# A two-layer graph kernel: the second product by one level of Strassen's algorithm, bias addition on GpSimd, 16 row tiles, and an explicit order of all steps

## The chip, the core and the metric

The kernel runs on one core of one Trainium2 chip. The metric is the device time of one execution in microseconds, as the median of several runs. A core has five engines that run side by side, each with its own in-order queue of instructions: TensorE (matmuls, results in PSUM), VectorE, ScalarE, GpSimd, and SyncE, which here only issues DMA transfers. Engines wait for each other through semaphores. In the profile they are PE (its weight loads are PEld), DVE, ACT, POOL and SP.

## What is computed

The input x has 32 batches of 512 rows by 1024 columns; adj is a 512x512 matrix; all is float32.

```python
h = jnp.maximum(_layernorm(x, axis=-1), 0.0)
x = x + _L0_gnn_ref(h, L0_gnn_wq, L0_gnn_wk, adj, L0_gnn_bm)
h = jnp.maximum(_layernorm(x, axis=-1), 0.0)
x = x + _L1_gnn_ref(h, adj, adj, L1_gnn_bias)
```

The first layer is an attention over the 1024 columns: scores are q[m] + k[n] through a leaky ReLU, a softmax over n, and the weighted sum of the columns, multiplied by adj and passed through a bias and a ReLU. The second is one dense product per batch, out[m, f] = sum over n of adj[n, m]^2 h[n, f], plus a bias per column f. The change concerns the second.

## The kernel before, in words

**Tiles.** A batch's 512 rows are four row tiles of 128 partitions by 1024 columns. They live in one pool, xp, with 18 buffers (ROWS). A batch takes twelve of them in the course of its life: four loads of x (load, L578), which become the normalised h in place and feed the first product; four reloads of x as y (reload, L583), which gather the residual sums and are stored at the end (L888); and four tiles of the second layer's h (relu, L613). A new tile waits until the buffer it is given is free: its last reader is done, and if it was stored, its store has landed.

**First layer.** value (L724) multiplies h by the transposed adjacency. Since the scores are a sum, the softmax sums are prefix sums over sorted columns: rank (L667, L672, L676, VectorE) counts each column's place, scatter (L736, L737, GpSimd) writes the columns in sorted order into a table in DRAM, fetch (L753) reads it back, stationary (L796, GpSimd), scan (L812) and sums (L821 to L828) make the prefix sums and write them back, and gather (L833, GpSimd) fetches for each column the three rows it needs. weigh (L858, ScalarE) and combine (L862, VectorE: sixteen 128x512 instructions per batch) put them together, and turn (L869, L871) transposes the result on TensorE and adds it to y on VectorE.

**Second layer.** stats (L591), norm and slopes make the layer norm of y, relu (L613) writes h. lift (L619, VectorE, four instructions) then adds the column bias to y. propagate (L876) makes eight results of 128x512 per batch (four row tiles c, two halves i of the columns), each a sum of four matmuls with the squared adjacency wsq (made once in square, L537). finish (L884, VectorE) adds each result and a per-row constant bm (which undoes the -bm that turn took as its lower limit) to y; after the second half of a row tile its store is issued on SyncE (L888).

**What sets the order.** Every function above is a step. A table (PLAN, with corrections for the first and last batches in FIRST and LAST) gives every step of every batch a time; the steps of all batches are sorted by it, and each engine's instructions stand in its queue in that order. Five or so batches are under way at once: one batch's propagate stands between another's scans and a third's values. PSUM has eight banks, one per result.

```python
for n, t in enumerate(times):
    t = s.b * T + t + shift + stretch * (t - mean)
    steps.append((t, len(steps), f, (s, *lead, *(args[n] if args else (n,)))))
...
steps.sort(key=lambda e: e[:2])
with tc.manual_schedule():
    for _, _, f, args in steps:
        f(*args)
```

Of the kernel before, what the change touches and what calls it, by code (L numbers as in the profile page):

```python
# [9 lines left out]
F32 = mybir.dt.float32  # L10
# [6 lines left out]
P = 128  # L17
# [8 lines left out]
ROWS = 18  # L26
QROWS = 4
PLAN = {
    "adjacency": (-988.26,),
    "biases": (-98.417,),  # L30
    "columns": (-36.55,),
    "combine": (
        258.562, 258.888, 261.232, 259.873, 259.273, 258.008, 255.401, 254.706, 263.584, 262.603,
        263.336, 256.739, 262.598, 262.619, 257.172, 258.38,
    ),
    "compare_mask": (-790.92,),
    "divide": (245.486,),
    "excess": (235.359,),
    "factors": (7.808,),
    "fetch": (33.445,),  # L40
    "finish": (320.504, 328.605, 338.372, 339.335, 347.583, 375.553, 352.541, 377.322),
    "from_rows": (59.35,),
    "gather": (219.377, 220.155, 219.449, 220.224, 220.347, 220.229, 219.664, 221.598),
    "later": (44.625,),
    "lift": (323.119, 320.65, 321.319, 325.518),
    "load0": (-153.915,),
    "load1": (-113.779,),
    "load2": (-165.384,),
    "load3": (-89.604,),
    "lower": (-8.757, 10.345, -12.887, -23.448, -21.118, -20.974, -1.148, 2.379),  # L50
    "masks": (-130.916,),
    "norm0": (-78.759,),
    "norm1": (284.555,),
    "pads": (-161.502, -74.73, -204.361, 23.867, -54.392),
    "propagate": (312.313, 317.412, 326.151, 316.354, 335.303, 344.312, 335.972, 347.511),
    "rank": (-14.187, -14.293, -17.198, -17.342, -15.511, -15.036, -11.325, -13.895),
    "reload0": (192.65,),
    "reload1": (238.382,),
    "reload2": (232.99,),
    "reload3": (257.454,),  # L60
    "relu0": (-61.287, -58.703, -61.202, -57.828),
    "relu1": (301.878, 303.027, 301.741, 302.05),
    "row": (-36.021,),
    "scan": (51.176, 57.633, 64.219, 81.673, 97.074, 108.292, 133.694, 146.062, 161.601),
    "scatter": (20.023, 15.884, 17.044, 17.539, 21.356, 19.535, 20.598, 20.763),
    "scores": (-41.613,),
    "slopes0": (-64.705,),
    "slopes1": (285.486,),
    "spread": (-28.707, -25.435, -27.151, -16.385, -9.829, -20.617, -16.323, -10.067),
    "square": (-559.865,),  # L70
    "stationary": (45.131, 68.681, 108.55),
    "stats0": (-97.083, -80.936, -91.631, -79.428),
    "stats1": (279.045, 280.054, 279.907, 280.042),
    "sums": (51.891, 59.593, 72.069, 86.019, 99.75, 116.792, 139.403, 150.307, 173.296),
    "to_rows": (-11.86, -7.955),
    "totals": (50.392,),
    "turn0": (264.575, 264.492, 264.401, 264.843),
    "turn1": (269.122, 269.027, 269.324, 268.845),
    "turn_adjacency": (-328.788,),
    "value": (-34.236, -39.683, -34.816, -23.667, -14.904, -27.47, -22.782, -17.741),  # L80
    "weigh": (250.503, 251.121, 249.656, 248.481, 251.121, 249.301, 250.914, 250.078),
    "weights": (41.352,),
}
FIRST = {
    "columns": (
        (-34.664, 0.5139), (-50.924, 3.8424), (-25.352, -0.3814), (5.756, -0.7592),
        (-3.834, -3.5685), (-13.836, 0.3613),
    ),
    "combine": (
        (-10.962, -0.1119), (-1.308, -0.1439), (3.109, -1.7623), (9.89, 2.7475), (4.44, -0.7933),  # L90
        (2.961, -1.451),
    ),
    "divide": (
        (-6.347, -0.8568), (2.891, -3.3805), (-4.843, -2.2912), (-14.719, 0.1095), (0.139, -0.7459),
        (-4.639, -1.4913),
    ),
    "excess": (
        (3.406, 3.0798), (0.53, -2.1584), (-5.407, -3.6123), (-5.253, 0.2855), (1.538, 1.0506),
        (-3.02, -0.7059),
    ),  # L100
    "factors": (
        (-39.948, -1.434), (8.997, -3.1502), (-4.905, 1.5535), (21.711, -1.2202), (-25.661, 2.8879),
        (13.506, 1.2709),
    ),
    "fetch": (
        (-7.266, -0.8474), (-8.348, -0.3577), (-7.803, -0.4204), (-12.929, 0.9352),
        (-3.76, -1.7209), (-5.744, 2.9838),
    ),
    "finish": (
        (-8.493, -0.4813), (6.16, 0.0186), (3.358, -0.186), (-1.573, -0.1421), (1.288, 0.2274),  # L110
        (-7.871, -0.1255),
    ),
    "from_rows": (
        (-0.341, 2.1537), (116.48, -0.09), (-35.198, 1.4406), (-25.171, -1.3726), (0.332, 0.6924),
        (-16.655, 0.2663),
    ),
    "gather": (
        (-5.507, 0.5725), (-4.646, -0.3848), (-17.558, -0.6343), (-8.351, -0.483), (5.293, 1.8179),
        (-2.911, -0.6571),
    ),  # L120
    "later": (
        (-10.16, 1.3573), (-2.311, -1.2079), (-2.744, 1.4084), (-11.928, 2.0169), (-8.624, -2.2893),
        (0.485, -2.4426),
    ),
    "lift": (
        (-13.784, -1.0616), (3.658, -0.7922), (-29.558, 1.5668), (-5.824, -1.5872), (1.316, 0.2108),
        (-13.838, -1.4015),
    ),
    "load0": (
        (-175.071, -1.0804), (-56.257, 0.2897), (-197.902, -2.8166), (2.16, -0.6659),  # L130
        (-45.079, 1.0239), (23.433, -0.0172),
    ),
    "load1": (
        (-99.914, 2.1645), (-71.298, -3.9416), (-78.407, 2.8558), (-85.073, 0.4063),
        (-18.406, -0.1573), (-28.218, 0.3374),
    ),
    "load2": (
        (-70.747, -1.2538), (-111.83, -0.5989), (-26.701, -0.4923), (-111.109, -0.0099),
        (-20.511, 0.9791), (15.469, 0.2457),
    ),  # L140
    "load3": (
        (-206.722, 1.2803), (-128.427, -0.9745), (-37.172, 1.9538), (-74.142, 0.1775),
        (-13.958, 1.1538), (-37.508, 0.7277),
    ),
    "lower": (
        (-27.213, -0.696), (-36.917, 0.5414), (-27.222, -0.2022), (-13.712, -0.526),
        (-10.212, -0.0938), (46.957, -1.0187),
    ),
    "norm0": (
        (-82.445, 1.5089), (-65.85, -1.4094), (-21.204, -0.8537), (-14.029, -0.5842), (1.32, 1.776),  # L150
        (1.134, -0.2082),
    ),
    "norm1": (
        (-3.753, -0.8553), (7.036, 1.1487), (-3.41, 0.1137), (10.96, 0.1134), (5.687, 1.1579),
        (-1.719, -1.6549),
    ),
    "propagate": (
        (-0.512, -0.1834), (1.688, 0.0269), (-2.93, -0.0228), (-0.493, -0.1178), (0.476, -0.1272),
        (0.797, -0.0815),
    ),  # L160
    "rank": (
        (-18.998, 0.7993), (-32.202, -0.2074), (-19.965, 1.145), (-3.668, -1.203),
        (-5.408, -1.0875), (2.158, -0.1924),
    ),
    "reload0": (
        (-78.853, -1.3542), (-2.901, -0.2085), (48.545, 0.1436), (11.898, 1.3227),
        (28.811, -1.2219), (-1.29, -0.8095),
    ),
    "reload1": (
        (-41.749, 0.1112), (-10.749, -0.6043), (11.812, -1.0105), (7.019, -0.2259),  # L170
        (-60.814, -0.4054), (-89.384, 1.1482),
    ),
    "reload2": (
        (5.935, 0.7012), (9.237, 1.9026), (-112.445, -1.6665), (29.821, 0.2364), (-22.535, -0.3722),
        (10.909, 1.7943),
    ),
    "reload3": (
        (-10.61, -1.1804), (-7.721, -1.5967), (-28.859, -3.3307), (-19.113, 0.0501),
        (-9.413, 0.4983), (-16.835, 0.7363),
    ),  # L180
    "relu0": (
        (-60.02, 1.4731), (-66.989, -0.4028), (-18.196, 0.1369), (-19.764, 0.0603), (3.168, 0.0151),
        (-1.522, 0.1367),
    ),
    "relu1": (
        (-11.851, 2.5102), (-0.995, 1.8084), (-17.155, -2.1914), (1.666, 2.1743), (4.982, -0.4455),
        (3.476, 0.1775),
    ),
    "row": (
        (-58.902, 0.8165), (-32.755, -3.2129), (-16.685, -0.2803), (-0.884, 2.3638),  # L190
        (-10.929, 0.751), (-15.002, 1.1386),
    ),
    "scan": (
        (-5.392, -0.0092), (-4.281, 0.0691), (-9.753, -0.1007), (-4.67, 0.0238), (-1.515, -0.0228),
        (-2.326, 0.0007),
    ),
    "scatter": (
        (-9.248, -0.2038), (-2.595, 1.766), (5.273, -0.6066), (-14.049, -0.0507), (0.917, 1.0603),
        (-5.17, -0.1987),
    ),  # L200
    "scores": (
        (-62.678, -1.1751), (-58.023, -2.2273), (-24.037, 0.8897), (-9.373, 1.8513),
        (-9.692, 0.3259), (-10.3, 1.643),
    ),
    "slopes0": (
# [765 lines left out]
```

## Time and profile before

| | |
|---|---|
| median of three runs | 2348.87 us (2348.57 to 2350.3) |
| the profiled execution | 2340.51 us, its span 2338.8 us |
| granted clock of TensorE | 0.994 on average |
| instructions | 27844 |
| DMA | 655.92 MB, mean 280 GB/s |
| HBM | 438.05 MB read, 215.99 MB written |

The profile is one execution. A row of the groups names the line, the engine, the operation and the tiles (out<-in) with their shapes and the number of instructions; then the busy time in us and the mean of one instruction in ns; then the engine's idle time just before these instructions, and who ended it. Instructions of one engine overlap a little at their ends, so the busy time of a group divided by its count is the pitch, somewhat below the mean. A row of the waits reads: who waited, for whom, us in total, times, the longest. In a timeline a row gives the start, the length in us, the engine and the instruction; equal ones that follow each other are one row with their count.

### The profile page before, as it was taken

How to read it: one execution, taken by the hardware profiler on the slowest of the kernel's cores; microseconds unless marked ns; L12 is line 12 of the kernel's file. 1: busy time of each engine (PE TensorE's matmuls, PEld its weight loads, DVE VectorE, ACT ScalarE, POOL GpSimd, SP SyncE). 2: the span in 40 equal slices, each digit the busy share in tenths (PEclk: the TensorE clock that was granted, in tenths of full speed). 3: DMA queues.
4: the chain of work that ended last, by engine and by line, in shares of the span. 5: the costliest groups of instructions: out<-in, count | busy, mean ns of one | idle time of the engine just before them, and what ended most of it. 6: DMA issues, size and time to landing. Idle time of an engine off the chain costs nothing.

```text
span 2338.8 us, 27844 instructions
## 1 busy us (share of the span) xinstructions
PE 2277.8 (97%) x7568; PEld 1001.3 (43%) x7568; DVE 1953.9 (84%) x4981; ACT 1445.1 (62%) x2821; POOL 740.0 (32%) x971
## 2 busy tenths in 40 slices
PE   7899999999999999999999999999999999999997
PEld 3334443444444444444444444444444444444343
DVE  6668897888898888898888898888988896899875
ACT  4677666565566665576665676665576656676530
POOL 2233323322323322324322323322323333334310
PEclk9999999999999999999999999999999999999998
DMA  5679878888888888888888888888787887787971
GB/s 194 236 272 332 286 250 290 299 295 280 271 295 293 306 284 294 267 298 294 304 283 293 270 299 294 303 292 299 251 311 262 313 301 280 259 296 274 328 291 78
DMA packets 205356, 655.92 MB, mean 280 GB/s; under 512 B 27504, under 2 KB 27632, under 8 KB 205200
## 3 DMA queue, kind: packets, MB, share of 16 engines
q1 hardware_dynamic: 141408, 360.37, 46.4%
q0 software_dynamic: 57344, 276.86, 30.8%
q10 hardware_dynamic: 6448, 16.92, 2.3%
q8 instruction: 61, 1.00, 0.2%
q14 instruction: 95, 0.78, 0.1%
HBM read 438.05 MB, written 215.99 MB: 280 GB/s over the span
## 4 chain that ended last, share of the span: by engine, by line
PE 85%; DVE 6%; DMA 4%; ACT 2%; issue 1%; POOL 1%; ACTq 0%; SPq 0%; DVEq 0%; POOLq 0%
PE pv L724 35%; PE pg L876 33%; PE sc L812 9%; PE tr L869 5%; PE pq L625 2%; DMA g<-td,idg 2%; DVE g L862 2%; DVE st L591 1%; PE sc L809 1%; POOL g L833 1%; ACT h L613 1%; DVE y L871 1%; DMA qd<-qr 1%; DVE junk L672 0%; ACT junk L683 0%
## 5 line engine op out<-in xcount | busy, mean ns | idle before, releaser
L876 PE MATMUL pg<-h,wsq 128*128 128x512 f32 x2048 | 905.3, 595 | 12.8 <-ACT h L613 12.8
L724 PE MATMUL pv<-wmT,x 128*128 128x512 f32 x2048 | 916.2, 598 | 0.0
L876 PEld LDWEIGHTS pg<-h,wsq 128*128 128x128 f32 x2048 | 384.2, 190 | 505.9 <-issue 464.3
L724 PEld LDWEIGHTS pv<-wmT,x 128*128 128x128 f32 x2048 | 377.1, 190 | 504.4 <-issue 442.7
L796 POOL TENSOR_TENSOR sm<-mask_a,wc 128x192 f32<-128x192 f32 x96 | 54.9, 572 | 1129.3 <-DVE wc L773 784.7
L821 ACT COPY vs<-sc 1x512 f32<-1x512 f32 x256 | 145.4, 568 | 374.8 <-PE sc L812 301.7
L862 DVE SCALAR_TENSOR_TENSOR g<-g,cf 128x512 f32<-128x512 f32 x512 | 360.9, 760 | 13.4 <-ACT g L858 10.6
L737 POOL DMA_INDIRECT td<-v,idx x256 | 290.5, 1135 | 236.0 <-POOL v L736 45.6
L683 ACT ACTIVATE junk<-qrow,qk 128x1024 uint8<-128x1024 f32 x256 | 294.1, 1149 | 11.9 <-DMA qrow<-qd 8.9
L833 POOL DMA_INDIRECT g<-td,idg x256 | 244.0, 953 | 125.2 <-issue 69.7
L812 PE MATMUL sc<-vs,sm 128*64 128x512 f32 x1024 | 265.9, 613 | 10.8 <-ACT vs L821 6.1
L884 DVE SCALAR_TENSOR_TENSOR y<-pg,bm_sb,y 128x512 f32<-128x512 f32 x256 | 186.0, 740 | 41.6 <-PE pg L876 26.8
L871 DVE SCALAR_TENSOR_TENSOR y<-tr,nbm,y 128x512 f32<-128x512 f32 x256 | 174.1, 742 | 38.5 <-PE tr L869 34.5
L824 ACT COPY t<-sc 128x512 f32<-128x512 f32 x288 | 168.3, 585 | 30.8 <-DMA td<-t 25.3
L672 DVE TENSOR_SCALAR_CACHE_REDUCE junk<-qrow,qk,cnt 128x512 uint8<-128x512 f32 (+6 forms) x224 | 180.4, 805 | 8.2
L667 DVE TENSOR_SCALAR_CACHE_REDUCE junk<-qrow,qk 128x512 uint8<-128x512 f32 (+6 forms) x224 | 165.4, 738 | 18.4 <-DMA qrow<-qd 13.3
L591 DVE BATCH_NORM_STATS2 st<-x 128x6 f32<-128x512 f32 x256 | 163.0, 678 | 17.7 <-DMA x<-in_x_dram 17.6
L858 ACT ACTIVATE g<-g,cf 128x512 f32<-128x512 f32 x256 | 163.2, 711 | 2.4 <-DVE cf L852 2.2
L613 ACT ACTIVATE h<-y,nmr,rstd 128x1024 f32<-128x1024 f32 x128 | 151.7, 1234 | 17.3 <-DMA out_dram<-y 9.4
L619 DVE TENSOR_TENSOR y<-y,bias_sb 128x1024 f32<-128x1024 f32 x128 | 151.3, 1213 | 12.0 <-ACT h L613 11.8
L591 DVE BATCH_NORM_STATS2 st<-y 128x6 f32<-128x512 f32 x256 | 159.3, 664 | 0.0
L731 ACT COPY v<-pv 128x512 f32<-128x512 f32 x256 | 139.0, 585 | 23.9 <-PE pv L724 9.9
(102 smaller groups left out, 1776.6 us busy)
## 6 DMA issues: line engine op xcount, KB each, us to landing
vs<-td SPq DMA_DIRECT2D x96, 792.0 KB
td<-t SPq DMA_DIRECT2D x576, 132.0 KB
x<-in_x_dram SPq DMA_DIRECT2D x128, 512.0 KB
y<-in_x_dram SPq DMA_DIRECT2D x128, 512.0 KB
out_dram<-y SPq DMA_DIRECT2D x128, 512.0 KB
qrow<-qd ACTq DMA_DIRECT2D x32, 512.0 KB
td<-v,idx POOLq DMA_INDIRECT x256, 4.9
g<-td,idg POOLq DMA_INDIRECT x256, 12.6
```

The lines of the kernel that those rows point to most:

```text
L591: nc.vector.bn_stats(st[:, i, :], s.x[c][:, ts(i, HALF)])
L613: nc.scalar.activation(h, s.x[c], AF.Relu, bias=s.nmr[:, c : c + 1], scale=s.rstd[:, c : c + 1])
L672: nc.vector.tensor_scalar(junk[:, j * P :], s.qrow[:, j * P :], qc, first, ALU.is_lt, ALU.add, accum_out=s.cnt[:, 1, j : j + 1],)
L683: nc.scalar.activation(junk, s.qrow, AF.Sign, bias=s.qk[:, 1, j : j + 1], accum_out=s.sgn[:, j : j + 1])
L724: nc.tensor.matmul(pv, s.h[c][:, ts(j, P)], wmT[:, c, :], start=(c == 0), stop=(c == NC - 1))
L737: i = nc.gpsimd.indirect_dma_start(tds[s.b % TABLES][:, :], bass.IndirectOffsetOnAxis(ap=s.idx[j // 4][:, j % 4 : j % 4 + 1], axis=0), v[: ...
L812: nc.tensor.matmul(p[ts(k, HP), :], m[:, k, :], s.vs[h][:, 0:C], start=True, stop=True)
L833: nc.gpsimd.indirect_dma_start(s.g[:, j, :], None, tds[s.b % TABLES].rearrange("(s k) w -> s k w", k=3), bass.IndirectOffsetOnAxis(ap=s.id ...
L862: nc.vector.scalar_tensor_tensor(r, s.g[:, j, k * W : k * W + C], s.cf[:, k, j : j + 1], r, ALU.mult, ALU.add)
L871: nc.vector.scalar_tensor_tensor(xh, pt, nbm[:, o : o + 1], xh, ALU.max, ALU.add)
L876: nc.tensor.matmul(pg, wsq[:, r, ts(c, P)], s.h[r][:, ts(i, HALF)], start=(r == 0), stop=(r == NC - 1),)
L884: nc.vector.scalar_tensor_tensor(xh, s.pg.pop((c, i)), bm_sb[:, c : c + 1], xh, ALU.add, ALU.add)
```

## The change

propagate no longer makes each 128x512 result from four matmuls. The 512x512 matrix, the rows and the column halves are split in two each, and Strassen's scheme in its form with shared sums makes the product from seven block products instead of eight. Each block product m is two half products u of two matmuls. square makes the combinations of the squared adjacency once (wmix, three of them; two blocks of wsq are overwritten). mix makes the combinations of h for every batch, in eight 128x512 subtractions on GpSimd, partly in place and partly in one more row tile, mx. Products 1, 6, 7 and 4 accumulate in one PSUM bank per u, products 5 and 3 in another, and finish reads the bank between them: seven instructions per u, four of which add bm. The store is a step of its own. lift goes from VectorE to GpSimd. ROWS goes from 18 to 16. PLAN, FIRST and LAST go, and a text (ORDER) names every step of the program in its order, two characters for each.

```diff
-ROWS = 18
+ROWS = 16
...
     def square(s):
         nc.gpsimd.tensor_tensor(wsq, s.adj, s.adj, ALU.mult)
+        a11, a21 = wsq[:, 0:2, 0 : C // 2], wsq[:, 0:2, C // 2 :]
+        a12, a22 = wsq[:, 2:4, 0 : C // 2], wsq[:, 2:4, C // 2 :]
+        s1, s2, s4 = wmix[:, 0], wmix[:, 1], wmix[:, 2]
+        nc.gpsimd.tensor_tensor(s1, a21, a22, ALU.add)
+        nc.gpsimd.tensor_tensor(s2, s1, a11, ALU.subtract)
+        nc.gpsimd.tensor_tensor(s4, a12, s2, ALU.subtract)
+        nc.gpsimd.tensor_tensor(a21, a11, a21, ALU.subtract)
+        nc.gpsimd.tensor_scalar(a22, a22, -1.0, None, ALU.mult)
+        forms.update({1: a11, 2: a12, 3: s4, 4: a22, 5: s1, 6: s2, 7: a21})
...
     def lift(s, c):
-        nc.vector.tensor_tensor(s.x[c], s.x[c], bias_sb, ALU.add)
+        nc.gpsimd.tensor_tensor(s.x[c], s.x[c], bias_sb, ALU.add)
...
+    def mix(s, k):
+        t, r = divmod(k, 2)
+        if k == 0:
+            s.mx = xp.tile([P, N], F32, tag="x", name=f"mx_{s.b}")
+        lo, hi = slice(0, HALF), slice(HALF, N)
+        d, h0, h1 = s.mx[:, ts(r, HALF)], s.h[r], s.h[2 + r]
+        out, one, two = (
+            (d, h0[:, hi], h0[:, lo]),
+            (h0[:, hi], h1[:, hi], h0[:, hi]),
+            (d, h1[:, hi], d),
+            (h1[:, lo], d, h1[:, lo]),
+        )[t]
+        nc.gpsimd.tensor_tensor(out, one, two, ALU.subtract)
+
+    def propagate(s, m, u):
+        row, i = {1: (0, 0), 2: (2, 0), 3: (2, 1), 4: (2, 0), 5: None, 6: None, 7: (0, 1)}[m] or (0, 0)
+        key = {1: 1, 6: 1, 7: 1, 4: 1, 5: 5, 3: 5, 2: 2}[m], u
+        if m in (1, 2, 5):
+            s.pg[key] = bank(f"pg_{s.b}_{m}_{u}")
+        for r in range(2):
+            data = s.mx[:, ts(r, HALF)] if m in (5, 6) else s.h[row + r][:, ts(i, HALF)]
             nc.tensor.matmul(
-                pg, wsq[:, r, ts(c, P)], s.h[r][:, ts(i, HALF)],
-                start=(r == 0), stop=(r == NC - 1),
-            )
...
+                s.pg[key], forms[m][:, r, ts(u, P)], data,
+                start=(m in (1, 2, 5) and r == 0), stop=(r == 1),
+                skip_group_check=True,
+            )
+
+    def finish(s, k, u):
+        key, c, i, last = (
+            (1, 0, 0, False), (2, 0, 0, True), (1, 0, 1, False), (5, 2, 1, True),
+            (1, 2, 1, False), (5, 0, 1, True), (1, 2, 0, True),
+        )[k]
+        xh = s.x[c + u][:, ts(i, HALF)]
+        if last:
+            nc.vector.scalar_tensor_tensor(
+                xh, s.pg[key, u], bm_sb[:, c + u : c + u + 1], xh, ALU.add, ALU.add
+            )
+        else:
+            nc.vector.tensor_tensor(xh, s.pg[key, u], xh, ALU.add)
+
+    def store(s, c):
+        nc.sync.dma_start(out[s.b, ts(c, P), :], s.x[c])
...
-    steps.sort(key=lambda e: e[:2])
+    names = list(lanes)
+    for code in ORDER.split():
+        for k in range(0, len(code), 2):
+            name, n = names[int(code[k : k + 2], 36)]
+            f, args = lanes[name, n].pop(0)
+            s, t = args[0], len(steps)
+            steps.append((t, len(steps), f, args))
```

In the middle of the new order (batches 8 to 20) each batch repeats the one before. A stretch of it, a step per word, the number after the point being the batch:

```
to_rows1.18 sums2.17 divide0.15 scatter6.18 propagate1.14 weigh4.15 scatter4.18 weigh7.15 combine8.15 propagate3.14 weigh6.15 load2.20 combine14.15 reload0.15 weigh5.15 scatter5.18 finish8.14 reload1.15 weigh3.15 combine10.15 propagate0.14 weigh0.15 combine11.15 mix0.14 weigh2.15 combine1.15 spread7.18 scan3.17 mix1.14 combine4.15
...
finish9.14 turn11.15 store1.14 propagate11.14 sums5.17 value3.19 finish11.14 reload3.15 fetch.18 turn03.15 turn13.15 propagate2.14
```

## The prediction

> **What bounds the kernel now.** I read the page's busy shares first, then the costliest groups, the busy time by stretch, the waits, and last the timeline of two engines where they meet.
>
> ```profile
> PE 2277.8 (97%) x7568; PEld 1001.3 (43%) x7568; DVE 1953.9 (84%) x4981; ACT 1445.1 (62%) x2821; POOL 740.0 (32%) x971
> ...
> L876 PE MATMUL pg<-h,wsq 128*128 128x512 f32 x2048 | 905.3, 595 | 12.8 <-ACT h L613 12.8
> ...
> L862 DVE SCALAR_TENSOR_TENSOR g<-g,cf 128x512 f32<-128x512 f32 x512 | 360.9, 760 | 13.4 <-ACT g L858 10.6
> ...
> L884 DVE SCALAR_TENSOR_TENSOR y<-pg,bm_sb,y 128x512 f32<-128x512 f32 x256 | 186.0, 740 | 41.6 <-PE pg L876 26.8 <-ACT t L824 14.5
> ...
> L619 DVE TENSOR_TENSOR y<-y,bias_sb 128x1024 f32<-128x1024 f32 x128 | 151.3, 1213 | 12.0 <-ACT h L613 11.8
> ```
>
> TensorE is busy for 97% of the span, and the second product (L876) is 905.3 us of it. The program has 1024 such matmuls, so each leaves two of the 2048 records: 0.884 us per matmul. VectorE is second. Busy over count gives its pitch: 0.705 us for a combine (L862), 0.727 for a finish (L884), 1.18 for a bias addition (L619).
>
> Now the middle, where the order repeats from batch to batch:
>
> ```profile
> 600.00:1200.00 600.00, 598.53 (x2038) 265.61 (x2035) 519.51 (x1311) 381.43 (x750) 196.30 (x258) 1.00 0.83 288
> 1200.00:1800.00 600.00, 600.00 (x1994) 263.31 (x1993) 518.77 (x1340) 386.27 (x755) 192.60 (x251) 1.00 0.83 291
> ```
>
> ```profile
> 1164.52 10.50 PE pg L876 x24
> ...
> 1234.74 10.50 PE pg L876 x24
> ```
>
> Columns: stretch, length, then busy time of PE, PEld, DVE, ACT and POOL, granted clock, DMA share, GB/s. TensorE is never idle at a clock of 1.00. In the chain of work the same group returns after 70.22 us: one batch. VectorE is busy 1038.28 of 1200 us, 60.8 per batch. Of its 9.4 idle us, the waits below make 7.3; 2.2 are gaps between its small steps, which stay.
>
> ```profile
> DVE den L790 <- PE pd L786: 66.5, 16, 4.4
> DVE y L871 <- PE tr L869: 18.5, 17, 1.8
> DVE y L884 <- ACT t L824: 14.5, 12, 1.9
> ```
>
> So VectorE needs 63.0 of the 70.2 us if nothing makes it wait. That is the number to watch.
>
> **TensorE.** Per batch 14 half products of two matmuls replace 8 of four: 28 for 32. Twelve matmuls (24 records) take 10.50 us, 0.875 each, so 3.5 us per batch go: 70.2 to 66.7, and 128 x 0.884 = 113 us in all. That is the ceiling of the gain.
>
> **VectorE.** Four bias additions leave (-4.73 us); finish grows from 8 to 14 instructions (6 x 0.727 = +4.36; the three per half without bias are plain additions from PSUM, nearest row L884). Net -0.4: 62.6 us undisturbed, against 66.7 of TensorE. Two things disturb it.
>
> **GpSimd, and what it does to VectorE.** GpSimd gets eight 128x512 subtractions (mix) and four 128x1024 additions (lift) per batch. Two rows are near, in the groups kept apart by shape:
>
> ```profile
> L796 POOL TENSOR_TENSOR sm<-mask_a,wc 128x192 f32<-128x192 f32 x96 | 54.9, 572 | 1129.3 <-DVE wc L773 784.7 <-PE sc L812 344.0
> ...
> L537 POOL TENSOR_TENSOR wsq<-adjn 128x2048 f32<-128x2048 f32 x1 | 3.6, 3601 | 5.1 <-DMA adjn<-in_adj_dram 5.1
> ```
>
> An undisturbed L796 takes 0.50 us; the line through 192 and 2048 columns gives 1.04 us for 512 and 1.89 for 1024. The Trainium skill (GPSIMD Engine Reference, 3.1) has 4497 ns for a 2048-column addition, a quarter more than this row; by it a mix is about 1.2 and a lift 2.3 us (estimates). I take the row, and keep the rule for the upper end. Per batch that is 8 x 1.04 + 4 x 1.89 = 15.9 us (18.8 by the rule), 509 us in all on an engine busy 740 of 2339: its time is there. The price is paid elsewhere:
>
> ```profile
> 2192.32 11.16 DVE L862 SCALAR_TENSOR_TENSOR g<-g,cf 128x512 f32<-128x512 f32 x15
> ```
>
> ```profile
> 2194.33 1.09 POOL L796 TENSOR_TENSOR sm<-mask_a,wc 128x192 f32<-128x192 f32 x1 [19.04 <-PE sc L812]
> 2195.38 0.95 POOL L796 TENSOR_TENSOR sm<-mask_b,wc 128x192 f32<-128x192 f32 x1
> 2196.30 0.95 POOL L796 TENSOR_TENSOR sm<-mask_a,wc 128x192 f32<-128x192 f32 x1
> 2197.21 0.95 POOL L796 TENSOR_TENSOR sm<-mask_b,wc 128x192 f32<-128x192 f32 x1
> ```
>
> Four GpSimd operations run beside fifteen combines. Theirs stretch from 0.50 to 0.95 us, and the combines take 11.16 us where undisturbed ones, 0.66 us apart, take 9.98: 0.3 us lost per collision. They take turns. L884 and L591, with one operand in SBUF, keep their 0.74 and 0.67 us beside L796. A 128x192 operation held VectorE for about 0.36 us of its 0.50 (after its release a combine still needed its 0.55); a 1.04 us mix then holds 0.9 and costs 0.8.
>
> In the new order all eight mixes stand between the combines: mix 0 to 3 wait behind three scatters (1.55 us each), which wait for an index that VectorE writes just before the combines. Some six of eight collide: 4.8 us. The lifts stand beside the rank steps, whose third instruction (L676) has two SBUF operands, and beside the small index steps: about 0.5 us each, 2 us. Together **6.8 us per batch**. Bounds: 0, were they all to fall beside finishes and statistics; 12 with every hold paid in full at the skill's rate.
>
> **The row tiles.** 18 buffers become 16, and a batch takes 13 (mx is new). Following the buffers in the built program: in batches 8 to 20 the fourth reload of y takes the buffer of the second y of the batch before. It has to wait until that y's store has landed, and it is queued on SyncE behind that store; the fetches of the sorted rows stand behind it. On VectorE the last finish of the stored y, then one turn, one finish, then the turn that needs the reload follow each other: 1.4 us of work beside two transfers. Behind that turn wait the rest of VectorE's queue and, for the next finish, TensorE. No such pair is in the middle of before (its nearest have 33 instructions or more between).
> Landing records of before: stores take 2.6 us alone, 4.0 beside one other, 5.6 in the median; reloads 4.1 alone, 4.6 beside a few, 5.7 in the median. Little else is in flight there: 3.9 + 4.6 + 0.1 = **8.6 us** (bounds 6.8 and 11.3).
> This closes a ring on VectorE alone: everything but those two steps, 62.6 - 1.4 = 61.2, plus 8.6 = 69.8 us per batch, plus the collisions.
>
> **The other edits.** The weight sums in square are five GpSimd operations at the start, some 5 us by L537, long before the first second product: nothing (5 us without that cover). Eight banks per batch become six: nothing, but below nothing possible. The order itself moves every queue; I cost it by the two rings only.
>
> **Sum.** For 13 batches: 69.8 + 6.8 = 76.6 for 70.2, +83 us. In the other 19 TensorE gives up 66 us, of which the collisions (19 x 6.8 = 129 us on a VectorE that idles some 220 us there, mostly at head and tail) and a few looser store-reload pairs take back about 50: -15. 2340.5 + 83 - 15 = 2409 for the profiled execution; the median of before is 8.4 us above its profiled one, so **2417 us**, 2.9% slower.
>
> **Rivals.**
> 1. *The collisions miss.* The ring is 69.8 without them, and only what stays under 0.4 us per batch leaves the middle as fast as before. If mixes run ahead of the combines (GpSimd idles over half the time) and the transfers come at their shortest (6.8), the ring is 68.0 and 1.5 us of collisions give 69.5: -9 in the middle, -50 at the ends, 2281 + 8 = **2290**. For it: the waits of L796 show GpSimd idle for 1129 us; against it: the scatters chained to VectorE's index. It decides at a sum of chain and collisions under 9 us per batch.
> 2. *TensorE stays the bound.* 2348.9 - 113 = **2236**. This needs VectorE under 66.7, which the ring excludes unless store and reload together land within 5.5 us; the shortest of before make 6.8.
> 3. *All is paid in full.* Long transfers (11.3) and 10 us of collisions: 82.5 per batch, +160, and nothing left at the ends: **2510** or more.
>
> **Chances.** The forecast 0.58, rival 1 0.24, rival 2 0.05, rival 3 0.13. The range 2270 to 2510 leaves out rival 2, the low edge of rival 1 and the far part of rival 3. About 0.2% is what a measurement of this kernel can tell from no change; some 0.04 falls within it, between the forecast and rival 1. Faster 0.27, slower 0.69. For the slower cases alone: 2370 to 2510.
>
> **What would show it.** In the profile after: L617 with 1792 records and about 792 us; TensorE idle in the middle; a VectorE wait of 5 to 9 us per batch before a turn, put down to the reload of y or the store; combines beside mixes at well over 0.74 us; a steady period near 76. If TensorE is above 97% in the middle, the rings were wrong; if the period is long without those two signs, something in the new order that I didn't cost.

## The result, and the profile after

The changed kernel takes 2760.57 us in the median (2757.87 to 2762.97) beside 2348.72 us of the kernel before: 1.1753 times as long, with a 95% interval of 1.1732 to 1.1773. The prediction had the sign and not the size: 2417 us, in a range of 2270 to 2510.

The page of the changed kernel, its busy shares and the row of granted clocks:

```profile
PE 2339.7 (85%) x7312; PEld 988.6 (36%) x7312; DVE 2336.4 (85%) x5045; ACT 1456.4 (53%) x2821; POOL 1321.0 (48%) x1360
...
PEclk8999899998999999999999999999899999999988
```

TensorE has 256 matmul records fewer and is still busy for 62 us more than before; VectorE has 64 instructions more and is busy for 382 us more. GpSimd's busy time went from 740 to 1321 us. In the middle (stretch, length, busy time of PE, PEld, DVE, ACT, POOL, granted clock, DMA share, GB/s):

```profile
1200.00:1800.00 600.00, 510.54 (x1605) 216.07 (x1604) 527.69 (x1103) 316.59 (x616) 285.47 (x294) 0.93 0.68 238
```

No engine is full: TensorE, which had 600 of 600 us here, has 511, at a clock of 0.93 instead of 1.00. The groups of the changed kernel, with different shapes kept apart (busy us, mean ns, then the idle time before):

```profile
L585 DVE SCALAR_TENSOR_TENSOR g<-g,cf 128x512 f32<-128x512 f32 x512 | 586.1, 1193 | 21.4 <-ACT g L581 11.0 <-ACT t L548 8.0 <-issue 0.8
...
L342 POOL TENSOR_TENSOR y<-y,bias_sb 128x1024 f32<-128x1024 f32 x128 | 301.8, 2374 | 147.3 <-ACT h L336 106.4 <-issue 25.3 <-DVE y L634 8.3
...
L399 DVE SCALAR_TENSOR_TENSOR junk<-qrow,qk,before 128x128 uint8<-128x128 f32 x256 | 180.7, 706 | 9.1
...
L608 POOL TENSOR_TENSOR mx<-h 128x512 f32<-128x512 f32 x64 | 80.2, 1275 | 9.6 <-DMA out_dram<-y 5.5 <-PE pv L447 3.6
...
L428 DVE TENSOR_SCALAR rk<-sgn 128x8 f32<-128x8 f32 x32 | 41.0, 1280 | 16.6 <-ACT junk L406 16.6
```

The combines (L585, before L862) went from 0.76 to 1.19 us, +225 us in sum. The rank steps' third instruction (L399, before L676 with 91.3 us) gained 89 us. L428, a 128x8 operation on one input, went from 0.17 us to 1.28: +36. None of these lines was touched by the change. The last two were, in the kernel before:

```profile
L676 DVE SCALAR_TENSOR_TENSOR junk<-qrow,qk,before 128x128 uint8<-128x128 f32 x256 | 91.3, 356 | 9.1
...
L705 DVE TENSOR_SCALAR rk<-sgn 128x8 f32<-128x8 f32 x32 | 5.4, 167 | 0.0
```

A mix takes 1.27 us and a lift 2.37, not the 1.04 and 1.89 of the prediction. The instructions with one operand in SBUF (finish L630, turn L594) kept their 0.74 us.

Who then waits for that, on TensorE (waited for: us in total, times, longest), and VectorE's own longest wait:

```profile
PE pg L617 <- DVE y L630: 205.3, 30, 14.2
PE pg L617 <- POOL mx L608: 67.3, 17, 5.7
```

```profile
DVE y L594 <- DMA y<-in_x_dram: 100.0, 25, 7.0
```

A half product that accumulates in a bank waits for the finish that reads the bank first; that finish stands in VectorE's queue behind combines which GpSimd holds. The timeline of the changed kernel shows one such place (start, length, engine, instruction):

```profile
1264.36 8.72 DVE L585 SCALAR_TENSOR_TENSOR g<-g,cf 128x512 f32<-128x512 f32 x4
...
1265.98 2.49 POOL L608 TENSOR_TENSOR mx<-h 128x512 f32<-128x512 f32 x2
...
1268.44 2.49 POOL L608 TENSOR_TENSOR h<-h,h 128x512 f32<-128x512 f32 x2
...
1270.89 0.50 POOL L519 TENSOR_TENSOR sm<-mask_a,wc 128x192 f32<-128x192 f32 x1
1271.36 0.50 POOL L519 TENSOR_TENSOR sm<-mask_b,wc 128x192 f32<-128x192 f32 x1
```

Four combines need 4 x 0.66 = 2.64 us undisturbed; here they take 8.72, so 6.08 are lost. GpSimd's series from the first mix to the last L519 lasts 1265.98 to 1271.86, 5.88 us. The loss is the whole series, and one of the four combines bears it: no combine gets in between two GpSimd operations that follow each other.

This is the common case, not the only one. In the records of the change, 50 unbroken series of two or more two-input GpSimd operations met a combine. In 41 of them GpSimd kept its pace and a combine stood until the series was through; in the other 9 GpSimd's operations were stretched and combines ended among them. What decides between the two was not found.

The lifts do the same to the index steps:

```profile
1330.67 4.73 POOL L342 TENSOR_TENSOR y<-y,bias_sb 128x1024 f32<-128x1024 f32 x2 [1.48 <-ACT h L336]
...
1333.12 2.31 DVE L428 TENSOR_SCALAR rk<-sgn 128x8 f32<-128x8 f32 x1
```

L428 ends only when the second lift is through, at 1335.4.

**Where the 418 us are.** divide has one reciprocal per batch. From that of batch 8 to that of batch 21, 13 batches of the repeated part, it is 912.9 us before and 1115.2 after: 70.2 and 85.8 per batch, +202 us. The rest of the span, the first and last batches, went from 1425.9 to 1642.0: +216. The prediction had +83 and -15.

### The profile page after: what moved, and what is told of

The parts are those of the page before. It is cut to its first block, busy times and chain, and to the rows that moved or that the text cites. A ratio compares the mean times of both kernels' runs of the same rounds, so it can differ in the third digit from the quotient of the medians.

```text
span 2757.2 us, 27996 instructions
## 1 busy us (share of the span) xinstructions
PE 2339.7 (85%) x7312; PEld 988.6 (36%) x7312; DVE 2336.4 (85%) x5045; ACT 1456.4 (53%) x2821; POOL 1321.0 (48%) x1360
## 5 line engine op out<-in xcount | busy, mean ns | idle before, releaser
L585 DVE SCALAR_TENSOR_TENSOR g<-g,cf 128x512 f32<-128x512 f32 x512 | 586.1, 1193 | 21.4 <-ACT g L581 11.0
L617 PE MATMUL pg<-h,wsq 128*128 128x512 f32 x1024 | 486.0, 611 | 17.3 <-DVE y L634 9.0
L519 POOL TENSOR_TENSOR sm<-mask_a,wc 128x192 f32<-128x192 f32 x96 | 50.4, 525 | 732.0 <-DVE wc L496 679.7
L342 POOL TENSOR_TENSOR y<-y,bias_sb 128x1024 f32<-128x1024 f32 x128 | 301.8, 2374 | 147.3 <-ACT h L336 106.4
L617 PE MATMUL pg<-mx,wmix 128*128 128x512 f32 x512 | 288.3, 701 | 83.7 <-POOL mx L608 67.3
L617 PE MATMUL pg<-h,wmix 128*128 128x512 f32 x256 | 171.0, 808 | 205.3 <-DVE y L630 205.3
L535 PE MATMUL sc<-vs,sm 128*64 128x512 f32 x1024 | 295.0, 628 | 33.4 <-ACT vs L544 14.2
L594 DVE SCALAR_TENSOR_TENSOR y<-tr,nbm,y 128x512 f32<-128x512 f32 x256 | 181.1, 746 | 150.9 <-DMA y<-in_x_dram 100.0
L617 PEld LDWEIGHTS pg<-h,wsq 128*128 128x128 f32 x1024 | 192.3, 195 | 255.3 <-issue 213.7
L630 DVE SCALAR_TENSOR_TENSOR y<-pg,bm_sb,y 128x512 f32<-128x512 f32 x256 | 188.7, 742 | 37.0 <-PE pg L617 30.2
L617 PEld LDWEIGHTS pg<-mx,wmix 128*128 128x128 f32 x512 | 106.6, 222 | 246.3 <-POOL mx L608 103.7
L399 DVE SCALAR_TENSOR_TENSOR junk<-qrow,qk,before 128x128 uint8<-128x128 f32 x256 | 180.7, 706 | 9.1
L395 DVE TENSOR_SCALAR_CACHE_REDUCE junk<-qrow,qk,cnt 128x128 uint8<-128x128 f32 (+6 forms) x224 | 180.5, 806 | 8.2
```

Source lines behind the costliest of these rows:

```text
L342: nc.gpsimd.tensor_tensor(s.x[c], s.x[c], bias_sb, ALU.add)
L395: nc.vector.tensor_scalar(junk[:, j * P :], s.qrow[:, j * P :], qc, first, ALU.is_lt, ALU.add, accum_out=s.cnt[:, 1, j : j + 1],)
L399: nc.vector.scalar_tensor_tensor(junk[:, ts(j, P)], s.qrow[:, ts(j, P)], qc, before, ALU.is_equal, ALU.mult, accum_out=s.cnt[:, 2, j : j + 1],
L535: nc.tensor.matmul(p[ts(k, HP), :], m[:, k, :], s.vs[h][:, 0:C], start=True, stop=True)
L585: nc.vector.scalar_tensor_tensor(r, s.g[:, j, k * W : k * W + C], s.cf[:, k, j : j + 1], r, ALU.mult, ALU.add)
L594: nc.vector.scalar_tensor_tensor(xh, pt, nbm[:, o : o + 1], xh, ALU.max, ALU.add)
```

## The experiments

The first two rows are the profiled executions of the result; each other time is of one execution, beside the kernel before on the same chip (2342 to 2348 us). "Middle" is the spacing of those 13 batches, "rest" the span without them.

| kernel | us | middle, us per batch | rest, us |
|---|---|---|---|
| before | 2340.5 | 70.2 | 1425.9 |
| the change | 2759.0 | 85.8 | 1642.0 |
| fill_mix | 2479.3 | 75.2 | 1500.3 |
| lift_dve | 2743.4 | 85.2 | 1633.5 |
| turn_late | 2754.0 | 86.1 | 1632.7 |
| psum_pairs | 2532.2 | 74.8 | 1558.5 |
| psum_lift | 2510.6 | 73.7 | 1551.4 |
| all_vector | 2567.3 | 78.4 | 1546.2 |
| mix_spaced | 2719.4 | 82.4 | 1646.3 |
| before_lift | 2367.2 | 70.2 | 1452.4 |
| order_alone | 2467.2 | 74.1 | 1502.4 |
| order_rows18 | 2441.7 | 74.1 | 1476.6 |

### The suspected cost taken away: mixes that read nothing, lifts back on VectorE

My theory after the result: GpSimd's series hold VectorE, VectorE's late finishes hold TensorE. The rival: the chain of store, reload and turn, which the prediction had put into its ring.

```diff
-        nc.gpsimd.tensor_tensor(out, one, two, ALU.subtract)
+        nc.gpsimd.memset(out, 0.25)
```

> The changed kernel, but the eight subtractions of mix are left out: GpSimd writes a constant into the same tiles at the same places, reading nothing. Collision theory (VectorE's combines stand still while GpSimd reads the row buffers): the combine group falls from 586 us to some 365, the steady batch from 85.3 to about 75, the time to 2440-2540. Rival, the row buffers (store, then reload, then a turn): combines may change but the wait of the turn grows in their place, the time stays above 2680. Rival, the new order and the half products that wait for finishes: TensorE's waits for finishes stay at over 200 us, the time stays above 2680.

2479.26 us, 280 less than the change. In fill_mix the combines are back near their old time, while the memsets still run on GpSimd, 0.53 us each:

```profile
L585 DVE SCALAR_TENSOR_TENSOR g<-g,cf 128x512 f32<-128x512 f32 x512 | 379.3, 790 | 22.2 <-ACT g L581 20.8
```

So GpSimd's mere activity doesn't hold the combines; that points to its reading. The edit takes away more than the reading, though: a memset lasts less than half as long as a mix and doesn't wait for h, so not all of the 280 us need be the reading's. The Trainium skill (SBUF — State Buffer, "Who interferes with whom") has this rule: a VectorE instruction with two inputs in SBUF contends with a GpSimd instruction that reads SBUF, not with one that only writes it; with at most one such input, and outside the modes in which VectorE uses two ports, it doesn't contend. Combines, finishes and turns agree here. L428 has one input and was held; whether it ran in such a mode no run here shows.

```diff
     def lift(s, c):
-        nc.gpsimd.tensor_tensor(s.x[c], s.x[c], bias_sb, ALU.add)
+        nc.vector.tensor_tensor(s.x[c], s.x[c], bias_sb, ALU.add)
```

> The changed kernel with the bias addition back on VectorE, at the same places of the order. Collision theory: VectorE takes on 4.7 us per batch and is freed of what the lifts cost it (third rank step 2.8, the index steps about 3): within 1.5% of 2760, the third rank step back from 706 to about 360 ns. If the lifts cost VectorE nothing, the time grows by 4.7 x 32 = 150 us; if GpSimd's own queue is what is late, it falls by over 3%.

2743.41 us, 0.6% less. L399 fell from 180.7 to 105.7 us and L428 from 41.0 to 8.0, for 161.6 us of lifts on VectorE. The combines kept their 586.6 us: the lifts are not what holds them. On the other side, the lift's move to GpSimd alone, in the kernel before:

> The kernel before, with the bias addition moved to GpSimd alone: no Strassen, the old order. Nothing is left out. The collision theory: 2.37 us per lift instead of VectorE's 0.6, and VectorE freed of 8 x 0.61 us but held for up to as long as the lifts run beside two-operand work; TensorE is busy 96 per cent there, and VectorE has 7 us per batch to spare, so within 1 per cent of the kernel before, 2335 to 2375 us. If a GpSimd operation cost VectorE only a collision of 0.3 us each: 2335 to 2350, no loss, and the two-operand operations beside it would keep their times.

2367.15 us, +0.9%, as the collision theory forecast. (A lift on VectorE is four instructions of 1.18 us per batch, not eight of 0.6 as the expectations have it; the sum is nearly the same.) L676 went from 91.3 to 131.6 us and the combines from 360.9 to 376.8. The middle stayed at 70.2, since TensorE is the bound there and VectorE had the time; the loss is in the first and last batches.

### The chain of store, reload and turn

The two turns that wait for the reload (turn 3 of each half) moved in the list to just before turn 2 of the first half.

> The changed kernel with the two turns that wait for the fourth reload moved behind the rank steps, to just before the next turns. If store and reload are a link of the ring on VectorE, the 100 us of waits on the reload go and the time falls by 70-100 us, to 2660-2690. If the wait only uses up time that VectorE has anyway, another wait takes its place and the time stays above 2730.

2754.04 us: another wait took its place. VectorE's waits in turn_late:

```profile
DVE qk L369 <- PE pr L364: 80.9, 19, 5.9
...
DVE y L594 <- DMA y<-in_x_dram: 16.6, 5, 5.3
```

The wait for the reload fell from 100 to 17 us, and that for the transposed scores, behind the products in TensorE's queue, rose from 19 to 81. The wait was exchanged, not removed, and the time stayed. So the wait at this place is not what sets the pace, unless the move itself made the new wait a link; that is not excluded.

### Another operand instead of another order: the running sum in PSUM

weigh writes the running sum of a row tile into a PSUM bank and both combines read it there; rows are combined in pairs.

```diff
-        r = s.g[:, j, 0:C]
-        nc.scalar.mul(r, r, s.cf[:, 0, j : j + 1])
+        s.r[j] = bank(f"r_{s.b}_{j}")
+        nc.scalar.mul(s.r[j], s.g[:, j, 0:C], s.cf[:, 0, j : j + 1])
...
-        r = s.g[:, j, 0:C]
+        r = s.r[j] if k == 1 else s.g[:, j, 0:C]
         nc.vector.scalar_tensor_tensor(
-            r, s.g[:, j, k * W : k * W + C], s.cf[:, k, j : j + 1], r, ALU.mult, ALU.add
+            r, s.g[:, j, k * W : k * W + C], s.cf[:, k, j : j + 1], s.r[j], ALU.mult, ALU.add
         )
...
```

> The changed kernel with the combines' running sum in a PSUM bank: weigh writes it there, both combines read it there, so each has one operand in SBUF. The sixteen stand in pairs per row group; nothing is left out. Collision theory: combines no longer stand still beside the mixes, group from 586 to 340-380 us, steady batch about 75, time 2440-2540. If what holds the combines is not their second operand in SBUF, the group stays above 500 us. Eight more banks per batch may make TensorE wait; then the combines are fast and the time is not.

2517.49 us. In this kernel two turns of batch 7 stood ahead of their combines, so that batch lacks terms. With the succession mended:

> Weigh writes the running sum of a row tile into a bank of PSUM and both combines read it there, so that a combine has one operand in SBUF instead of two; rows are combined in pairs, in the order in which the turns ask for them. Nothing is left out (the first kernel of this kind had two turns of one batch ahead of their combines). If the time of the change is VectorE held by GpSimd's series: as that kernel, 2500 to 2535 us, combines 0.75 us. If the earlier gain came from the misplaced turns: 2600 us or more.

2532.18 us, and the combines of psum_pairs, with the real mixes beside them:

```profile
L585 DVE SCALAR_TENSOR_TENSOR r<-g,cf,r 128x512 f32<-128x512 f32 x256 | 191.7, 749 | 19.2 <-ACT r L581 19.1
...
L585 DVE SCALAR_TENSOR_TENSOR g<-g,cf,r 128x512 f32<-128x512 f32 x256 | 191.1, 746 | 7.7
```

0.75 us each instead of 1.19, with one operand moved out of SBUF, and 227 us less than the change. (The combines' new succession and eight more banks per batch are in this too; they were not tried alone.) TensorE's largest wait fell with it, from 205.3 us in sum, so late finishes and held combines belong together:

```profile
PE pg L617 <- DVE y L630: 44.3, 11, 9.2
```

Next, the lifts on VectorE as well, and then the turns moved too:

> The kernel with combines on PSUM, and the bias addition back on VectorE, eight operations of 0.6 to 0.7 us per batch. Nothing is left out. GpSimd then does only mixes, weights and copies. If what is left of the loss (about 5.6 us per batch) is the lifts' series holding VectorE's small index operations, the exchange is about even, 5.6 saved for 5 paid, less what the tail of the small operations delays: 2440 to 2520 us, the small index operations back to the times of the kernel before (the first of them 5 to 10 us in sum instead of some 40). If the rest is the wait for the reloaded tiles or TensorE at its lowered clock: 2510 to 2540, no gain.

2510.64 us, another 22 us. L399 is down to 101.3 us and L428 to 14.6. The time lies where the two ranges of the expectation overlap, so it doesn't decide between them.

> The same with the two late turns that wait for a reloaded tile moved to just before the turn after them. Nothing is left out. With the collisions gone the store, reload and turn chain may at last be a link of its own (its wait was about 87 us in sum): if so 60 to 90 us less than the same kernel without the move. If another wait takes its place, as with the two-operand combines, within 20 us of it.

2519.44 us. Again the reload's wait was only exchanged (26 us instead of 91, and 81 for the scores instead of 18).

### Taking turns, or a series that keeps VectorE out

```diff
         nc.gpsimd.tensor_tensor(out, one, two, ALU.subtract)
+        nc.gpsimd.memset(idle, 0.0)
```

> The change, with a small memset of GpSimd (128 x 256 into a tile of its own, about 0.3 us) after each mix. Nothing is left out. Memsets did not hold VectorE, so each mix is now followed by a space in which VectorE can start. If GpSimd keeps VectorE out only while its two-input operation runs: four mixes in a series hold one combine 1.3 us each instead of one combine 5 us, the sum of the combines stays near 586 us and the longest fall from 6 us to about 2.3; time within 2 per cent of the change, 2710 to 2810. If VectorE, once it is in, makes the mix wait: mixes stretch from 1.27 us to 1.5 to 2 us and combines lose less, below 500 us in sum. If GpSimd's queue as a whole keeps it out, memsets too: combines above 640 us, 2800 or more.

2719.35 us: 40 us less although GpSimd does 80 us more. The timeline of mix_spaced:

```profile
1260.59 4.44 DVE L586 SCALAR_TENSOR_TENSOR g<-g,cf 128x512 f32<-128x512 f32 x3
1261.08 0.31 POOL L610 MEMSET idle<- 128x256 f32 x1
1261.35 1.46 POOL L609 TENSOR_TENSOR h<-mx,h 128x512 f32<-128x512 f32 x1
...
1262.76 0.30 POOL L610 MEMSET idle<- 128x256 f32 x1
1263.03 1.46 POOL L609 TENSOR_TENSOR h<-mx,h 128x512 f32<-128x512 f32 x1
```

One combine starts in each memset, and the mix behind it takes 1.46 us instead of 1.27: now they do take turns. Three combines end in 4.44 us beside two mixes; in the change four needed 8.72 beside four mixes and two L519. The combines' sum fell only from 586 to 558 us, between the two forecasts: a combine is still held by one mix at a time.

The whole of it on VectorE (mixes and lifts):

> The change with its mixes and its bias addition on VectorE instead of GpSimd, combines as they are. Nothing is left out. GpSimd then holds VectorE nowhere but at weights and copies. A mix should take as long as a combine, 0.7 us, so eight are 5.6 us per batch, and the bias addition 5.1. Collision theory: VectorE 62.6 + 5.6 + 5.1 = 73 us per batch undisturbed, against 74.8 in the change, the long combines gone: 2560 to 2680, faster than the change though VectorE does more. If the collisions were not what holds the change back, the 10.7 us more per batch make it slower than the change, 2900 or more.

2567.31 us, 7% less than the change with more work on VectorE. Combines 0.75 us, L399 0.36. A mix took 0.88 us in its first form, more than I expected, and 0.68 in the three others.

### What is left: the order, the row tiles, or Strassen's product

psum_lift has no long combines and no long index steps, and still loses 165 us. The order alone: the list of the change with the plain product's 32 matmuls in the products' places, lifts on VectorE, no mixes.

> The explicit order and 16 row tiles alone: the order of the change with the second product computed as in the kernel before (32 matmuls, no mixes, eight finishes, all in the places where the seven products' matmuls and finishes stand) and the bias addition on VectorE. Nothing is left out. It tells how much of the 165 us that the kernel with combines on PSUM and lifts on VectorE still loses to the kernel before is the order's and the 16 tiles'. If the loss is Strassen's and GpSimd's: steady batches of 70.2 to 71 us and 2345 to 2390. If the order's first and last batches cost the rest (some 100 us by the spacing of the batches): 2420 to 2480. If the wait for the reloaded tiles also bounds the steady batches: 2480 or more.

2467.17 us, 125 us over the kernel before on the same chip. It is not the order alone in every respect: sixteen pairs of matmuls stand in fourteen places that were meant for the other product, and without mx a batch takes twelve row tiles instead of thirteen. The middle of order_alone, and its first wait on TensorE:

```profile
1200.00:1800.00 600.00, 579.18 (x1912) 246.98 (x1911) 494.76 (x1274) 369.93 (x719) 175.60 (x244) 1.00 0.78 277
```

```profile
PE tr L582 <- DVE g L575: 30.9, 36, 2.5
```

TensorE idles for 21 of 600 us where it idled for none. Over eight batches of the middle, by the matmul records:

| us per batch | period | TensorE busy | idle | of the busy time: second product |
|---|---|---|---|---|
| before | 70.2 | 70.2 | 0.05 | 27.7 |
| order_alone | 74.1 | 71.4 | 2.7 | 27.7 |
| psum_lift | 73.4 | 68.8 | 4.6 | 24.8 |
| the change | 85.8 | 73.2 | 12.7 | 29.2 |

In order_alone the idle time stands before transposes that wait for a combine (1.6) and before scans (1.1); the other 1.2 us are longer transposes and scans. The seven products do give up 2.9 us (psum_lift), and 1.9 us more of idle time and longer scans (9.55 us for 8.79) take most of that back.

Is it the 16 row tiles?

```diff
-ROWS = 16
+ROWS = 18
```

> The explicit order with the plain second product and lifts on VectorE (2467 us, steady batches of 74.1 us), with 18 row tiles instead of 16. Nothing is left out. In it VectorE waits 6.6 us per batch at a turn for the reloaded tile, whose load waits for a row tile that an earlier store sets free. If the 16 tiles are what bounds that order: the wait goes, steady batches come down to 70.2 to 71 us and the time to 2370 to 2420. If it is the order of the steps: within 15 us of 2467.

2441.74 us, in neither of the two ranges: the middle didn't move (74.1 us per batch), and the rest is 26 us shorter, 23 of them before the middle. The wait for the reload is still there with two row tiles more. Between 600 and 1800 us it was 78.5 us in order_alone, and here it is:

```profile
DVE y L584 <- DMA y<-in_x_dram: 80.4, 14, 7.8
```

So in this order the reload isn't late for want of a free row tile. The other reason that the prediction gave, its place behind the store in SyncE's queue, was not tried apart.

> The same order with the plain second product and 16 tiles, and the two turns that wait for a reloaded tile moved to just before the turn after them. Nothing is left out. If VectorE's waiting at these turns is a link of the loop: 2380 to 2420. If the loop runs through TensorE as well, as in the change, another wait takes its place: 2450 to 2475.

2474.62 us: the reload's wait fell from 117 to 25 us, that for the scores rose from 22 to 109. The wait was exchanged here too.

> Strassen's product with combines on PSUM and lifts on VectorE (2511 us, steady batches of 73.3 us), with 17 row tiles; the room comes from one buffer less for the rows of sums on their way to the table (one instead of two, which may cost ScalarE up to 4 us per row of sums where it is late). Nothing is left out. If row tiles bound what is left of the loss: 2400 to 2470. If the order does: 2500 or more.

2603.72 us, and it tells nothing of row tiles: the missing buffer cost more than I had allowed, ScalarE waited 319 us for the rows of sums to be written.

### Strassen's product in the old order

These kernels leave out the block sums of the matrix and add another resident tile in place of the bias, so the amounts of work are the same and the values are not.

> Strassen's seven products in the order of the kernel before (its table of times, 18 row tiles; the fourteen half products, mixes and finishes spread over the time in which the eight products stood), bias addition on VectorE. To make room for a tile of its own for mx, the sums of blocks of the matrix are left out (plain blocks are used in their place) and the bias addition adds another resident tile, so that the amounts of work are the same and the values are not. It tells whether the loss without collisions was the new order's. Mixes on GpSimd still hold the combines by up to 11 us per batch. VectorE before is 63.0 us per batch; it gets six finishes, 4.2 us, and 5 to 11 us of held combines: 72 to 78 us per batch in the middle, 2400 to 2560 in all. If mixes fall beside other work here: 68 to 70 us per batch, 2290 to 2340.

> The same with the combines' running sum in PSUM, so that GpSimd's mixes do not hold them. VectorE 63.0 + 4.2 = 67.2 us per batch, TensorE 70.2 less the 2.9 us that the products gave up in the other kernel without collisions, 67.3. If order and collisions were the whole of the loss: 67.5 to 69.5 us per batch in the middle, 2270 to 2335 in all, faster than the kernel before. If a wait of its own (finishes of one PSUM bank between products, ScalarE's running sums ahead of the scans) stays: 70 to 73 us per batch, 2345 to 2430.

2930.22 and 2921.64 us. Neither expectation held. In strassen_old_order the combines took 0.77 us: in these places the mixes hardly hold them, and the loss is another one. TensorE in strassen_old_order_psum:

```profile
PE pg L899 <- DVE y L916: 302.7, 150, 7.6
PE pg L899 <- DVE y L912: 85.7, 24, 9.2
```

Products of one bank wait for the finish between them, and VectorE in turn waits for the products (194 and 123 us at its finishes). The plain product has no such read between its matmuls. With the distances of the change's own order:

> As the last kernel (Strassen's products in the old order, running sums in PSUM; the sums of blocks and the bias values replaced by resident tiles, the amounts of work the same), but with the products, mixes, finishes and stores in the succession and at the distances that they have in the change's own order, stretched over 48 instead of some 40 units of the old table's 80.6 per batch. In the last kernel TensorE waited 303 us for a finish that stood between two products of one bank. If that closeness was its loss: that wait falls below 120 us and the time to 2340 to 2600. If the old places do not suit the chain of products and finishes at all: above 2700.

> The same, stretched over 54 units. If the distance decides, this one is faster than the last by some tens of us; if other waits do (row tiles held longer, loads that come later), it is as fast or slower. For Strassen to gain what TensorE gives up it would have to come to 2270 to 2335 us.

3089.81 and 2933.86 us. The two waits together, 388 us above, became 388 and 303. The wider spacing is 156 us faster than the narrower one, so distance counts, but no faster than the kernel above. The old places don't suit this chain at any distance tried; whether another order would let Strassen's product gain its 2.9 us per batch was not settled.

## Why the prediction was right and wrong

- **What TensorE gives up: right in kind.** 256 matmul records less, as forecast. In psum_lift the product is 2.9 us per batch shorter, for 3.5 forecast. In the change itself it is 1.5 us longer (29.2 for 27.7): its 1792 records take 945 us, not 792.
- **The collisions: the step that failed, by its rule and its rate.** "They take turns", 0.3 us per collision, came from one place where four short operations ran beside fifteen combines; "some six of eight collide: 4.8 us" and 2 us for the lifts made 6.8. The same trace held the other case. Ten GpSimd series met combines in it: in five they took turns, in five a combine stood until the end. One of these five:

```profile
1810.38 5.17 DVE L862 SCALAR_TENSOR_TENSOR g<-g,cf 128x512 f32<-128x512 f32 x6
...
1813.34 0.52 POOL L796 TENSOR_TENSOR sm<-mask_a,wc 128x192 f32<-128x192 f32 x1
...
1813.81 0.52 POOL L796 TENSOR_TENSOR sm<-mask_b,wc 128x192 f32<-128x192 f32 x1
```

  Neither GpSimd operation is stretched, and six combines take 5.17 us where 5 x 0.66 + 0.74 = 4.04 were due: 1.13 us lost beside a pair of 0.99. Shown in its place for the change: in 41 of 50 series VectorE is held until the series ends. VectorE is busy 382 us more, where its own edits made it 13 us less: 395 / 32 = 12.3 us per batch instead of 6.8. Of these, 7.0 are the combines' (beside 10.1 us of mixes), 2.8 L399's, 1.1 L428's, and the rest is spread over the small steps. The bound of 12 "with every hold paid in full" met this number by luck: mixes and lifts last 19.6 us per batch, and not all of it is paid. Nor is the loop longer by the holds alone: freeing the combines of their 7.0 us (psum_pairs) brought the middle from 85.8 to 74.8, 11.0 us, with TensorE's wait for the finishes down as well.
- **The duration of GpSimd's operations: wrong row.** I took 1.04 and 1.89 us from the line through L537, which multiplies a tile by itself, and put aside the 2048-column figure of the Trainium skill (GPSIMD Engine Reference, 3.1), from which I had estimated 1.2 and 2.3. Measured: 1.27 and 2.37. The sums of weight blocks in square, which run before any combine and have two different inputs, show it too, with 1.26 us for 512 columns:

```profile
L254 POOL TENSOR_TENSOR wmix<-wsq 128x512 f32<-128x512 f32 x1 | 1.3, 1263 | 0.1
```

  Whether it is the two equal inputs that make L537 the faster one was not tried apart.
- **Which instructions collide: too few.** I had the ones with two operands in SBUF and the small index steps at 0.5 us each. L428 has one input and no more than eight columns, and took 2.31 us in the place shown above, 1.28 in the mean.
- **The chain of store, reload and turn: the wait is there, that it is a link was not shown.** 5 to 9 us per batch were forecast before a turn; it is 5.2 in the middle. But three kernels in which those turns were moved (turn_late, psum_lift_late, order_late) were as slow, and two more row tiles didn't end the wait (order_rows18). The sum "69.8 plus the collisions" most likely added a wait that overlaps another one. That the middle without collisions is 73.7, close to 69.8, is no support for it.
- **"The order itself moves every queue; I cost it by the two rings only": the second step that failed.** The order with the plain product costs 125 us, of which 3.9 us per batch in the middle (50 us) and 77 us in the first and last batches; 26 us of the latter are the row tiles'.
- **The ends: -15 us forecast, +216 measured.** I counted on VectorE's idle time there to hide collisions. In psum_lift, without them, the rest of the span is 1551 us, in the change 1642: collisions cost 91 us there. The other 125 belong to the order and the row tiles (77 us in order_alone) and to the chain of products and finishes, which was not tried alone.
- **The rivals.** "All is paid in full" came nearest, and by its collisions; its other half, transfers of 11.3 us, was not seen (the wait for the reload is 5.2 us). It ended at 2510 because it left the ends unhurt and the order unpriced.

From kernel to kernel the 412 us (2348.7 to 2760.6) come as: order and 16 row tiles 125, Strassen's product in it 43 (order_alone to psum_lift, with mixes and PSUM sums), lifts on GpSimd 22 (psum_lift to psum_pairs), mixes beside two-operand combines 227 (psum_pairs to the change), less some 5 between chips. Another succession gives other shares: the lifts taken from the change first are worth 16. No kernel tried was faster than the kernel before.

## What to carry to other kernels

Before moving elementwise work to GpSimd, list what VectorE does beside it: each of its instructions with two operands in SBUF, and small one-input ones too, can be held for the whole length of an unbroken GpSimd series, so price the series and not the operation, and look for every place of the trace where the two meet, not for one; an operand in PSUM removed that price at no cost in VectorE's time. When an order is replaced, time the new order with the old work first: here that alone was 30% of the loss. And a wait seen in the trace is a term of the sum only if moving it away shortens the loop.

## What the runs showed of the hardware

- GpSimd's two-input operations that follow each other mostly let no combine in (6.08 us lost beside a series of 5.88; so in 41 of 50 series of the change, while in 9 they took turns); with a memset of 0.3 us between them, one combine started in each space.
- GpSimd's memsets, which read nothing, left the combines at 0.79 us.
- The granted TensorE clock fell together with TensorE's busy share: 0.994 on average before, 0.984 in order_alone, 0.962 in psum_lift, 0.923 in the change, down to 0.909 where TensorE was busy 79% of the span (strassen_old_order_48). Which of the two draws the other was not tried apart.
